# Softmax inverses sent through DRAM as 16 to a partition, more weight sums in the first attention, and block sums stored from ACT's queue

## The chip, the cores and the metric

The kernel runs on one core of one Trainium2 chip. The metric is device time in microseconds (us) of one execution, as the median of several. The core has a matrix engine (TensorE, PE in the profile), three engines for elementwise work (VectorE or DVE, ScalarE or ACT, GpSimd or POOL) and SyncE (SP), which here only issues transfers. Each engine runs its own instructions in order. DMA transfers can be issued by SP, ACT or POOL and run on 16 DMA engines. SBUF is the on-chip memory of 128 partitions, PSUM the accumulators of TensorE, DRAM the memory outside.

## What is computed

All data are float32. Layer 0 is an attention block over four images of 1024 channels by 1024 tokens, with 16 heads of 64; layer 1 is a bottleneck of three convolutions with batch norms and a residual.

```python
# layer 0
qkv = (x @ w_qkv.T + b_qkv).reshape(B, N, 3, nh, hd)
q, k, v = (qkv[:, :, 0], qkv[:, :, 1], qkv[:, :, 2])
q = _apply_rope(q, cos, sin)
k = _apply_rope(k, cos, sin)
q = _rmsnorm(q.reshape(B, N, inner), q_norm_w).reshape(B, N, nh, hd)
k = _rmsnorm(k.reshape(B, N, inner), k_norm_w).reshape(B, N, nh, hd)
scores = jnp.einsum('bqhd,bkhd->bhqk', q, k) * hd ** (-0.5)
attn = jax.nn.softmax(scores, axis=-1)
ctx = jnp.einsum('bhqk,bkhd->bqhd', attn, v).reshape(B, N, inner)
out = _rmsnorm(ctx @ w_proj.T, norm_out_w) + residual
# layer 1
out = jax.nn.relu(_bn(_conv(x, w1, b1, 1, 0), g1, be1))
out = jax.nn.relu(_bn(_conv(out, w2, b2, 1, 1), g2, be2))
out = _bn(_conv(out, w3, b3, 1, 0), g3, be3)
out = jax.nn.relu(x + jax.nn.softplus(residual_scale)[0] * out)
```

## The kernel before

**Stages.** For each image b (0 to 3): project Q, project K, project V, attention, project the context (Y), normalise and store to DRAM. The first convolution of layer 1 is interleaved at the end; the 3x3 convolution (Winograd form) and the third follow. The order on PE, POOL, DVE and ACT is written out by hand: what the program issues in sequence runs in that sequence on each engine. SP's order is arranged by the framework around the waits.

**Strassen sums of weights.** The projections save matmuls by a Strassen-Winograd scheme, which needs sums of blocks of the weights. Q and K of image 0 use one level (`project`): `operands` (L224) loads four 128x512 blocks, makes four sums on DVE (L231 to L234), uses them, and stores the sums to DRAM (L237), as `wd`. All others use two levels (`project2`, L432): their second-level sums are read from DRAM (`wd2`), seven parts for each of WQ, WK, WV and WP. They have to be made once before they are first used: `prepare` (L380) and, for first-level blocks, `prepare_blocks` (L396) load four 128x512 pieces, and a later `make` does four DVE operations of 0.69 us on them and issues four stores from POOL's queue.

**Where these sums are placed.** Beside a projection, `weight_parts(parts, first, step, lag, alloc)` (L935) schedules part i's loads, from POOL's queue, at product number first + i*step, and its `make` lag products later. A product is a group of matmuls; `after(n, step)` runs a step n products on. In the first attention, a list `todo` of such items is worked off: `extra_step` makes the item loaded two steps ago and loads the next, from SP's queue, into four of eight pieces of a ring. In image 3 the same place is taken by the five steps of `filters` (L887 to L915), which make Winograd filter sums: each is a DVE sum (L901), an ACT multiply by 0.5 (L902) and two further DVE operations.

**Attention.** `attention` (L740) is called for the two halves c of the query tokens; each goes over eight pairs of heads hp. For each pair: 32 score matmuls into three PSUM buffers (L757), eight exps on ACT (L764), seven additions on DVE that sum the exps over key blocks (`den`, L766 and L768), 32 matmuls with V (`cx`, L774), and a copy of the result into q's place by ACT (L779). After it come, in this order on DVE: means (L737) where an inverse is ready, a rope turn of K (L694) while some are still waiting, an extra step. After an odd pair eight matmuls with ones (`dn`, L800) sum `den` over the partitions for the two pairs. The reciprocal of `dn` is taken at the start of the next pair (`inverses`, L804 to L815): 128x512 on DVE, of which each row repeats 32 times; four rows go to DRAM (`dens`, a range check reads them at the end), and eight transfers spread the inverses inside SBUF to where `mean_of_v` multiplies them into q at the end of the next odd pair.

**The rule for an extra step** is one at most for each pair, and none beside a rope turn unless the list has become as long as the pairs that are left:

```python
left = (NCH - c) * NHP - hp - 1
turn = bool(waiting)
if turn:
    next_waiting()
if extra and (not turn or len(extra) >= left):
    extra.pop(0)()
```

When attention begins, two rope turns are still waiting in image 0 and four in the others (`rest(leave=...)`, L1014).

Of the kernel before, what the change touches and what calls it, by code (L numbers as in the profile page):

```python
# [11 lines left out]
F32 = mybir.dt.float32  # L12
# [6 lines left out]
P = 128  # L19
B, C, H, W = 4, 1024, 32, 32  # L20
N = H * W
NT = C // P
HD = 64
NHP = C // (2 * HD)
CH = 512
NCH = N // CH
# [8 lines left out]
WQ, WK, WV, WP, W1 = 0, NFB, 2 * NFB, 3 * NFB, 4 * NFB  # L35
# [26 lines left out]
NH = NT // 2  # L62
NG = NT // 2
QH = P // 4
# [21 lines left out]
def program(ctx, tc, x, wblk, w2, w3, vecs, cos, sin, out, bad):  # L86


    nc = tc.nc
# [63 lines left out]
    with tc.tile_pool(name=f"st{u}", bufs=2) as st, ExitStack() as s:  # L153
# [48 lines left out]
        def temp(name):  # L202
            return tmp.tile([P, CH], F32, tag="tmp", name=name)

        def big_temp(name):
            return big.tile([P, N], F32, tag="big", name=name)
# [8 lines left out]
        def flat(t):  # L215
            return t.rearrange("p a b -> p (a b)")
# [7 lines left out]
        def operands(base, g, name):  # L224


            at = base // NT * NG + g
            a11, a12 = (block(base, g, ih, f"{name}_1{ih}") for ih in range(2))
            a21, a22 = (block(base, g + NG, ih, f"{name}_2{ih}") for ih in range(2))
            s1 = chunk(f"w_{name}_s1")  # L230
            nc.vector.tensor_tensor(s1, a21, a22, ALU.add)  # L231
            nc.vector.tensor_tensor(a21, a11, a21, ALU.subtract)
            nc.vector.tensor_tensor(a11, s1, a11, ALU.subtract)
            nc.vector.tensor_tensor(a12, a12, a11, ALU.subtract)  # L234
            spend(4 * TT)
            for o, t in enumerate((a11, s1, a21, a12)):
                nc.gpsimd.dma_start(wd[at, o], flat(t))  # L237
            return [a11, s1, a21, a12, a22]


# [8 lines left out]
        def after(n, step):  # L249
            later.append((pace["at"] + n, step))  # L250
# [486 lines left out]
            nc.vector.tensor_tensor(cx, cx, w, ALU.mult)  # L737
            nc.gpsimd.tensor_scalar(cx, cx, col("bv", hp), None, ALU.add)  # L738

        def attention(b, c, q_all, k_all, v, probs_, late, ready, extra, slow):  # L740


            at = half[c]
            sums_ = []
            for hp in range(NHP):
                n = f"{b}_{c}_{hp}"
                if late:
                    late.pop(0)()
                rows = shifts(q_all, k_all, n, hp, c) if bad is None else None
                probs = []  # L750
                d_ = acc.tile([P, 2, CH], F32, tag="tot", name=f"den_{n}")
                for t in range(N // P):
                    p = probs_[:, t]
                    sc = bank("sc", f"sc_{n}_{t}")
                    for j in range(2):
                        d = slice(j * HD, (j + 1) * HD)
                        nc.tensor.matmul(  # L757
                            sc[:, j], k_all[d, hp, t * P : (t + 1) * P], q_all[d, hp, at],
                            start=True, stop=bad is not None,
                        )  # L760
                    if bad is None:
                        for j in range(2):
                            nc.tensor.matmul(sc[:, j], ones[0:1, :], rows[j], start=False, stop=True)
                    nc.scalar.activation(p, sc, AF.Exp)  # L764
                    if t == 1:
                        nc.vector.tensor_tensor(d_, probs[0], p, ALU.add)  # L766
                    elif t > 1:
                        nc.vector.tensor_tensor(d_, d_, p, ALU.add)  # L768
                    probs.append(p)
                o = bank("cx", f"cx_{n}")  # L770
                for t in range(N // P):
                    for j in range(2):
                        h0 = (2 * hp + j) * HD
                        nc.tensor.matmul(  # L774
                            o[j * HD : (j + 1) * HD, :], v[:, t, h0 : h0 + HD], probs[t][:, j],
                            start=(t == 0), stop=(t == N // P - 1),
                        )

                nc.scalar.copy(q_all[:, hp, at], o)  # L779
                sums_.append(d_)  # L780
                if hp % 2 == 1:
                    for r in ready:
                        mean_of_v(q_all, *r)
                    ready.clear()
                if slow:
                    slow.pop(0)()

                left = (NCH - c) * NHP - hp - 1
                turn = bool(waiting)
                if turn:  # L790
                    next_waiting()
                if extra and (not turn or len(extra) >= left):
                    extra.pop(0)()
                if hp % 2 == 0:
                    continue
                dn = bank("dn", f"dn_{n}")
                for i, d_ in enumerate(sums_):
                    for j in range(2):
                        q = slice((2 * i + j) * QH, (2 * i + j + 1) * QH)
                        nc.tensor.matmul(dn[q, :], ones[:, :QH], d_[:, j], start=True, stop=True)  # L800
                sums_ = []
                late.append(lambda *a, n=n, hp=hp, dn=dn: inverses(b, c, hp, n, dn, ready))

        def inverses(b, c, hp, n, dn, ready):  # L804
            r = temp(f"rec_{n}")
            nc.vector.reciprocal(r, dn)  # L806
            k = 2 * ((b * NCH + c) * NHP + hp - 1)
            if bad is not None:
                nc.sync.dma_start(dens[k : k + 4, :], r[::QH, :])
            w = big_temp(f"inv_{n}")  # L810
            for i in range(2):
                for j in range(4):
                    q = slice((2 * i + j // 2) * QH, (2 * i + j // 2 + 1) * QH)
                    nc.sync.dma_start(w[j * QH : (j + 1) * QH, half[i]], r[q, :])
                ready.append((c, hp - 1 + i, w[:, half[i]]))  # L815

        def o_norm(b, total, ys):
# [117 lines left out]
        def weight_parts(parts, first, step, lag, alloc):  # L935

            for i, part in enumerate(parts):
                after(first + i * step, lambda part=part: after(lag, part(alloc, nc.gpsimd)))

        def pieces_of(tile, cols=NCH):  # L940

            at = deque(tile[:, i, h] for i in range(tile.shape[1]) for h in half[:cols])

            def alloc(name):
                at.rotate(-4)
                return [at[i] for i in range(-4, 0)]

            return alloc
# [28 lines left out]
        for b in range(B):  # L977
# [8 lines left out]
            if b == 0:  # L986
                unused = kp.tile([P, NT, N], F32, tag="k", name="unused")
                parts = blocks_of(WV) + [parts_of[WV][k] for k in (0, 1, 6, 2)]
                weight_parts(parts, 8, 2.4, 4, pieces_of(unused))
            elif b == 1:  # L990
                weight_parts([parts_of[WK][k] for k in (4, 5)], 8.5, 3.5, 3.5, pieces_of(room[:, : NT // 2, :]))
            tq = qk_proj(b, WQ, xs[b], ts[b], "bq", q_all, "q", w1 if b == 0 else None, two, True)
            rope(b, q_all, tq, eps_q, HD / C, None, "q", b == 0)
            k_all = kp.tile([P, NT, N], F32, tag="k", name=f"k_{b}")
# [3 lines left out]
            if b == 0:  # L998
                parts = [parts_of[WV][k] for k in (3, 4, 5)] + [parts_of[WQ][k] for k in (0, 1)]
                weight_parts(parts, 2, 4.5, 4, pieces_of(room))  # L1000
            elif b == 1:
                weight_parts([parts_of[WK][6]], 11, 0, 3.5, pieces_of(room[:, : NT // 2, :]))
            tk = qk_proj(b, WK, xs[b], ts[b], "bk", k_all, "k", None, two)
            rope(b, k_all, tk, eps_rms, 1.0 / C, (wqk_other, wqk), "k")
            v = room
            if b == 0:
                two2 = [None, None, in_place(xs[b], ts[b], room, True)]

                t3 = pieces_of(xs[b][:, :NH, half[1]], 1)
                for k, at, free in ((6, 11, pieces_of(ts[b][1], 1)), (2, 14.5, t3), (3, 18.5, pieces_of(ts[b][1], 1))):  # L1010
                    weight_parts([parts_of[WQ][k]], at, 0, 3.5, free)
            project2(b, 1, WV, *two2[2], b == 0, v, True, "v", lambda c: None)

            rest(leave=4 if b > 0 else 2)  # L1014
# [2 lines left out]
            todo = []  # L1017
            if b == 0:
                todo = blocks_of(WP) + [parts_of[WP][k] for k in (0, 1, 6, 2, 3, 4, 5)]
                todo += [parts_of[WQ][k] for k in (4, 5)] + [parts_of[WK][k] for k in (0, 1)]  # L1020
            made = []

            def extra_step():
# [7 lines left out]
                extra_step()  # L1031
            if b == B - 1:
                extra = filters()
            late, ready = [], []

            def add_residual(f, b=b - 1):
                nc.gpsimd.dma_start(
# [4 lines left out]
            slow = [lambda: None] * 3 + [lambda f=f: add_residual(f) for f in range(NT)] if b > 0 else []  # L1042
            probs_ = xp.tile([P, N // P, 2, CH], F32, tag="x", name=f"p_{b}")
            for c in range(NCH):
                attention(b, c, q_all, k_all, v, probs_, late, ready, extra, slow)
            psum_for("proj")
            room = v_room(f"to_{b}")
            tc_ = [
# [30 lines left out]
                for i in range(NT):  # L1079
                    after(8 + 1.5 * i, lambda i=i: read_back(1, (i,)))  # L1080
            if b == 0:
                weight_parts([parts_of[WK][k] for k in (2, 3)], 6, 7, 4, pieces_of(room[:, 3 * NT // 4 :, :]))
            yt[b] = kp.tile([P, NT, N], F32, tag="k", name=f"y_{b}")
            two = (2, *in_place(q_all, tc_, yt[b], False), True)
            if b + 1 < B:
# [356 lines left out]
```

## Time and profile before

| | |
|---|---|
| median of 3 runs | 2709.47 us (2709.33 to 2710.42) |
| the profiled execution, as timed | 2709.99 us |
| its span, first to last instruction | 2708.20 us |
| TensorE's granted clock, mean | 0.995 |
| DVE reciprocal L806, 128x512 | 3.35 us, 32 times |
| DVE L766 and L768, sums of exps of one pair | 1.20 + 6 x 1.23 us |
| DVE L694, one rope turn | 1.28 + 1.31 us |
| DVE L737, one mean | 0.69 us, 64 times |
| ACT L779, a 128x512 copy | 0.59 us |
| ACT L764, one exp | 1.04 us |
| SP's wait at L809 for the reciprocal | 503.7 us in 25 times |
| SP's loads at L378 waiting for stores into wd2 | 97.9 us in 40 times |

A row of the list of groups gives an engine's busy time and the mean of one instruction. The list of waits gives how long an engine stood still in front of a line, and what came last of what it waited for; an idle engine that is not the bound costs nothing. The timeline gives single instructions, or runs of equal ones, with their starting times. Image 0's Q, K and V take the first 298 us, the first attention lasts to 533 us, and image 3's begins at 2038 us.

### The profile page before, as it was taken

To read this page: it belongs to the slowest core of one execution; us is meant where nothing else is said; L and a number is where in the kernel's file an instruction comes from. 1 tells how busy PE (TensorE), PEld (TensorE's weight loads), DVE (VectorE), ACT (ScalarE), POOL (GpSimd) and SP (SyncE) were. 2 spreads that over 40 slices of the span, in tenths; PEclk is the share of its full clock that TensorE was granted. 3 is DMA by queue.
4 is the path that set the end of the run, shared out by engine and by line. 5 is a ranking of instruction groups with operands and counts; after the bars stand their busy time and mean duration, and the time that the engine had idled before them with its cause. 6 is when DMAs were issued, how large, how long until landed. Compare 5 with 4: busy or idle time off the path is not lost. (4 is left out here: it accounts for less than half of the span.)

```text
span 2708.2 us, 32563 instructions
## 1 busy us (share of the span) xinstructions
PE 2669.3 (99%) x11410; PEld 1659.0 (61%) x11410; DVE 2169.5 (80%) x2516; ACT 1096.1 (40%) x1520; POOL 452.6 (17%) x552
## 2 busy tenths in 40 slices
PE   9999999999999999999999999999999999999997
PEld 4448533488888333688886333888884335746843
DVE  4577899998887977888878877987888878646987
ACT  2222455523342555333343555233525553312266
POOL 2562222322011211100111211100111211000000
PEclk9999999999999999999999999999999999999999
DMA  7897755587677341456765420665783314662165
GB/s 272 317 306 214 230 154 165 167 269 246 197 203 213 62 92 32 148 152 222 188 189 144 88 54 17 214 205 173 189 233 79 75 36 132 196 240 86 63 227 209
DMA packets 245964, 453.54 MB, mean 167 GB/s; under 512 B 28384, under 2 KB 117264, under 8 KB 245792
## 3 DMA queue, kind: packets, MB, share of 16 engines
q1 hardware_dynamic: 203568, 310.72, 36.5%
q0 software_dynamic: 42224, 140.63, 19.6%
q8 instruction: 94, 1.54, 0.2%
q14 instruction: 78, 0.64, 0.1%
HBM read 316.71 MB, written 96.78 MB: 153 GB/s over the span
## 5 line engine op out<-in xcount | busy, mean ns | idle before, releaser
L768 DVE TENSOR_TENSOR den<-den,p 128x1024 f32<-128x1024 f32 x384 | 470.5, 1225 | 40.7 <-DVE den L768 0.9
L764 ACT ACTIVATE p<-sc 128x1024 f32<-128x1024 f32 x512 | 476.3, 1043 | 55.0 <-PE sc L757 54.8
L757 PE MATMUL sc<-q,k 64*128 64x512 f32 x2048 | 457.7, 596 | 0.0
L757 PEld LDWEIGHTS sc<-q,k 64*128 64x128 f32 x2048 | 189.9, 186 | 265.6 <-issue 121.2
L774 PE MATMUL cx<-p,to 128*64 128x512 f32 x1536 | 340.2, 595 | 0.0
L774 PEld LDWEIGHTS cx<-p,to 128*64 128x64 f32 x1536 | 106.0, 137 | 228.3 <-issue 228.3
L738 POOL TENSOR_SCALAR q<-q,vec 128x512 f32<-128x512 f32 x64 | 127.0, 1989 | 559.2 <-DVE q L737 559.2
L453 PE MATMUL p_v<-w_v,x 128*128 128x256 f32 x928 | 210.8, 380 | 1.3 <-DVE x L424 1.3
L458 PE MATMUL p_y<-q,w_y 128*128 128x256 f32 x928 | 210.1, 380 | 1.1 <-DMA w_y<-wdf 1.1
L458 PEld LDWEIGHTS p_y<-q,w_y 128*128 128x128 f32 x928 | 175.9, 190 | 28.5 <-issue 4.8
L453 PEld LDWEIGHTS p_v<-w_v,x 128*128 128x128 f32 x928 | 176.9, 191 | 26.8 <-DVE x L424 2.1
L779 ACT COPY q<-cx 128x512 f32<-128x512 f32 x64 | 37.5, 587 | 356.9 <-PE cx L774 356.9
L458 PE MATMUL p_k<-to,w_k 128*128 128x256 f32 x672 | 154.8, 384 | 4.7 <-ACT to L547 4.7
L458 PE MATMUL p_q<-to,w_q 128*128 128x256 f32 x672 | 152.5, 380 | 0.7 <-ACT q L512 0.6
L458 PEld LDWEIGHTS p_k<-to,w_k 128*128 128x128 f32 x672 | 127.9, 192 | 26.3 <-ACT to L547 7.1
L458 PEld LDWEIGHTS p_q<-to,w_q 128*128 128x128 f32 x672 | 127.2, 190 | 20.2 <-ACT q L512 1.9
L766 DVE TENSOR_TENSOR den<-p 128x1024 f32<-128x1024 f32 x64 | 76.5, 1195 | 77.3 <-ACT p L764 77.3
L806 DVE RECIPROCAL rec<-dn 128x512 f32<-128x512 f32 x32 | 107.2, 3352 | 20.6 <-PE dn L800 20.6
L774 PE MATMUL cx<-p,rq 128*64 128x512 f32 x512 | 113.4, 595 | 0.0
L1346 PE MATMUL c<-h,w 128*128 128x512 f32 x256 | 110.3, 592 | 0.9 <-ACT h L1248 0.9
L700 POOL DMA_DIRECT2D k<-ks x64 | 56.1, 1036 | 278.2 <-ACT p L764 111.0
L453 PE MATMUL p_v<-w_v,t 128*128 128x256 f32 x384 | 92.0, 385 | 3.6 <-DMA w_v<-in_wblk_dram 3.6
(444 smaller groups left out, 4188.0 us busy)
## 6 DMA issues: line engine op xcount, KB each, us to landing
w_v<-wd2f SPq DMA_DIRECT2D x112, 256.0 KB
w_y<-wd2f SPq DMA_DIRECT2D x112, 256.0 KB
w_q<-wd2f SPq DMA_DIRECT2D x84, 256.0 KB
w_k<-wd2f SPq DMA_DIRECT2D x84, 256.0 KB
x<-in_x_dram SPq DMA_DIRECT2D x64, 256.0 KB
q<-qs POOLq DMA_DIRECT2D x64, 256.0 KB, 5.7
k<-ks POOLq DMA_DIRECT2D x64, 256.0 KB, 4.5
inv<-rec SPq DMA_DIRECT2D x256, 64.0 KB
```

The lines of the kernel that those rows point to most:

```text
L453: nc.tensor.matmul(o[:, q].rearrange("p (g f) -> p g f", g=2), r[:, i, q * P : (q + 1) * P], wt[:, :, i, :], skip_group_check=True, **at,)
L458: nc.tensor.matmul(o[:, q], wt[:, q, i, :], r[:, i, :], skip_group_check=True, **at)
L700: nc.gpsimd.dma_start(dst[i::2, f, :], other[1 - i :: 2, :], accum_op=ALU.add)
L738: nc.gpsimd.tensor_scalar(cx, cx, col("bv", hp), None, ALU.add)
L757: nc.tensor.matmul(sc[:, j], k_all[d, hp, t * P : (t + 1) * P], q_all[d, hp, at], start=True, stop=bad is not None,)
L764: nc.scalar.activation(p, sc, AF.Exp)
L766: nc.vector.tensor_tensor(d_, probs[0], p, ALU.add)
L768: nc.vector.tensor_tensor(d_, d_, p, ALU.add)
L774: nc.tensor.matmul(o[j * HD : (j + 1) * HD, :], v[:, t, h0 : h0 + HD], probs[t][:, j], start=(t == 0), stop=(t == N // P - 1),)
L779: nc.scalar.copy(q_all[:, hp, at], o)
L806: nc.vector.reciprocal(r, dn)
L1346: nc.tensor.matmul(os[i], w3t[k][f // NH][:, f % NH, :], h2[b, k][:, half[c]], start=(k == 0), stop=(k == NPT - 1),)
```

## The change

1. `inverses`: except for the last pair of an image (c = 1, hp = 7), where the code is as before, `dn` is copied to SBUF by ACT, not inverted; its four distinct rows go to DRAM, and from there come back as 128x16 (`few`). At the end of the same even pair (`half_done`) DVE inverts these, they go back to DRAM, and eight transfers broadcast them to 32 partitions each (`spread`).
2. The extra steps are spread evenly over the 15 slots of the 16 pairs of an attention, beside rope turns too. The first attention has 20 items for 15: WQ 3 and WK 6, 2, 3, 4 come in. With 20 items slots 0, 3, 6, 9 and 12 have two steps each. The five filter steps of image 3 come at slots 0, 3, 6, 9, 12.
3. Fewer parts beside projections: none beside Q and K of image 1, two beside V of image 0 (three before), one beside Y of image 0 (two before).
4. The four stores of `operands` come one product later, and from ACT's queue.

```diff
             spend(4 * TT)
-            for o, t in enumerate((a11, s1, a21, a12)):
-                nc.gpsimd.dma_start(wd[at, o], flat(t))
+
+            def keep():
+                for o, t in enumerate((a11, s1, a21, a12)):
+                    nc.scalar.dma_start(wd[at, o], flat(t))
+
+            after(1, keep)
             return [a11, s1, a21, a12, a22]
...
                     ready.clear()
+                if half_done:
+                    half_done.pop(0)()
                 if slow:
                     slow.pop(0)()
 
-                left = (NCH - c) * NHP - hp - 1
-                turn = bool(waiting)
-                if turn:
+                if waiting:
                     next_waiting()
-                if extra and (not turn or len(extra) >= left):
+                slots = NCH * NHP - 1
+                for _ in range(len(extra) - steps_in_all * max(slots - 1 - c * NHP - hp, 0) // slots):
                     extra.pop(0)()
...
+        half_done = []
+
         def inverses(b, c, hp, n, dn, ready):
+
+
             r = temp(f"rec_{n}")
-            nc.vector.reciprocal(r, dn)
             k = 2 * ((b * NCH + c) * NHP + hp - 1)
-            if bad is not None:
+            if (c, hp) == (NCH - 1, NHP - 1):
+                nc.vector.reciprocal(r, dn)
                 nc.sync.dma_start(dens[k : k + 4, :], r[::QH, :])
+                spread(c, hp, n, ready, [r[q * QH : (q + 1) * QH, :] for q in range(4)])
+                return
+            nc.scalar.copy(r, dn)
+            nc.sync.dma_start(dens[k : k + 4, :], r[::QH, :])
+            few = st.tile([P, 4 * CH // P], F32, tag="few", name=f"few_{n}")
+            rows = dens[k : k + 4, :].rearrange("r (a t) -> (r a) t", t=4 * CH // P)
+            nc.sync.dma_start(few, rows)
+
+            def invert():
+                nc.vector.reciprocal(few, few)
+                nc.sync.dma_start(rows, few)
+                spread(c, hp, n, ready, [dens[k + q, :].partition_broadcast(QH) for q in range(4)])
+
+            half_done.append(invert)
+
+        def spread(c, hp, n, ready, rows):
             w = big_temp(f"inv_{n}")
             for i in range(2):
                 for j in range(4):
-                    q = slice((2 * i + j // 2) * QH, (2 * i + j // 2 + 1) * QH)
-                    nc.sync.dma_start(w[j * QH : (j + 1) * QH, half[i]], r[q, :])
+                    nc.sync.dma_start(w[j * QH : (j + 1) * QH, half[i]], rows[2 * i + j // 2])
                 ready.append((c, hp - 1 + i, w[:, half[i]]))
...
-            elif b == 1:
-                weight_parts([parts_of[WK][k] for k in (4, 5)], 8.5, 3.5, 3.5, pieces_of(room[:, : NT // 2, :]))
             tq = qk_proj(b, WQ, xs[b], ts[b], "bq", q_all, "q", w1 if b == 0 else None, two, True)
...
-            elif b == 1:
-                weight_parts([parts_of[WK][6]], 11, 0, 3.5, pieces_of(room[:, : NT // 2, :]))
             tk = qk_proj(b, WK, xs[b], ts[b], "bk", k_all, "k", None, two)
...
-                t3 = pieces_of(xs[b][:, :NH, half[1]], 1)
-                for k, at, free in ((6, 11, pieces_of(ts[b][1], 1)), (2, 14.5, t3), (3, 18.5, pieces_of(ts[b][1], 1))):
-                    weight_parts([parts_of[WQ][k]], at, 0, 3.5, free)
+                weight_parts([parts_of[WQ][k] for k in (6, 2)], 11.5, 6.5, 4, pieces_of(ts[b][1], 1))
...
-                todo += [parts_of[WQ][k] for k in (4, 5)] + [parts_of[WK][k] for k in (0, 1)]
+                todo += [parts_of[WQ][k] for k in (3, 4, 5)] + [parts_of[WK][k] for k in (0, 1, 6, 2, 3, 4)]
...
-                weight_parts([parts_of[WK][k] for k in (2, 3)], 6, 7, 4, pieces_of(room[:, 3 * NT // 4 :, :]))
+                weight_parts([parts_of[WK][5]], 8, 0, 4, pieces_of(room[:, 3 * NT // 4 :, :]))
```

More of the change, by code (lines that the diff above doesn't have):

```diff
@@ L738, in mean_of_v, with attention @@
             nc.gpsimd.tensor_scalar(cx, cx, col("bv", hp), None, ALU.add)
-        def attention(b, c, q_all, k_all, v, probs_, late, ready, extra, slow):
+        def attention(b, c, q_all, k_all, v, probs_, late, ready, extra, slow, steps_in_all):
             at = half[c]
@@ L1033, in program @@
                 extra = filters()
-            late, ready = [], []
+            late, ready, steps_in_all = [], [], len(extra)
             def add_residual(f, b=b - 1):
@@ L1044, in program @@
             for c in range(NCH):
-                attention(b, c, q_all, k_all, v, probs_, late, ready, extra, slow)
+                attention(b, c, q_all, k_all, v, probs_, late, ready, extra, slow, steps_in_all)
             psum_for("proj")
```

## The prediction

> **What bounds the kernel now.** I read the busy table first, then TensorE's waits, then the stages that these waits name on the timelines, each engine apart.
>
> ```profile
> PE 2669.3 (99%) x11410; PEld 1659.0 (61%) x11410; DVE 2169.5 (80%) x2516; ACT 1096.1 (40%) x1520; POOL 452.6 (17%) x552
> ```
>
> TensorE is busy for all but 39 us, and the change leaves its instructions and their order alone. Only the gaps, and the slow matmuls behind a gap, can move. In the list of TensorE's waits (total, times, longest) the reader is to see five that matter:
>
> ```profile
> PE pa_q L298 <- DMA x<-in_x_dram: 5.9, 1, 5.9
> PE p_k L458 <- ACT to L547: 4.7, 6, 2.4
> PE p_v L453 <- DMA w_v<-in_wblk_dram: 3.6, 1, 3.6
> PE pa_k L298 <- DVE w_k_3b L233: 2.0, 1, 2.0
> PE p_q L458 <- DMA w_q<-wdf: 0.8, 2, 0.6
> PE pa_k L298 <- DVE w_k_2b L233: 0.6, 1, 0.6
> ```
>
> On TensorE's timeline (start, length, shape, count) a gap has a second price: the row behind it runs slower.
>
> ```profile
> 163.49 3.60 PE L298 MATMUL pa_k<-t,w_k_1b 128*128 128x512 f32 x8
> 187.13 5.40 PE L298 MATMUL pa_k<-t,w_k_3b 128*128 128x512 f32 x8 [1.99 <-DVE w_k_3b L233]
> 278.28 3.78 PE L453 MATMUL p_v<-w_v,t 128*128 128x256 f32 x8 [3.59 <-DMA w_v<-in_wblk_dram]
> 1333.23 1.89 PE L458 MATMUL p_k<-to,w_k 128*128 128x256 f32 x8
> 326.61 2.18 PE L800 MATMUL dn<-den,ones 128*32 128x512 f32 x8
> 357.07 1.07 PE L800 MATMUL dn<-den,ones 128*32 128x512 f32 x8
> ```
>
> Eight matmuls of 512 columns take 3.60 at pace and 5.40 after an idle 1.99; eight of 256 take 1.89 and 3.78. The first dn of image 0 takes 2.18 where the next takes 1.07: it already waits inside for its second operand. VectorE explains it, and what stands in front of the K sums:
>
> ```profile
> 182.15 0.69 DVE L387 TENSOR_TENSOR rq<-rq 128x512 f32<-128x512 f32 x1 [5.73 <-DMA rq<-in_wblk_dram]
> 319.81 7.87 DVE L768 TENSOR_TENSOR den<-den,p 128x1024 f32<-128x1024 f32 x6
> 2052.66 1.28 DVE L694 SCALAR_TENSOR_TENSOR ks<-k,wqk_other,sinT 128x1024 f32<-128x1024 f32 x1
> 2053.97 1.28 DVE L694 SCALAR_TENSOR_TENSOR k<-k,wqk,cosT 128x1024 f32<-128x1024 f32 x1
> 2053.17 7.44 ACT L764 ACTIVATE p<-sc 128x1024 f32<-128x1024 f32 x8 [0.47 <-PE sc L757]
> 298.00:533.00 235.00, 234.93 (x1090) 84.07 (x1088) 221.27 (x203) 129.83 (x145) 65.98 (x82) 1.00 0.54 164
> ```
>
> The last row is the first attention: length, busy time of PE, weight loads, DVE, ACT, POOL, clock, DMA share, GB/s. VectorE has 14 us to spare in 235 there, TensorE nothing.
>
> **What the Trainium skill says.** "TensorE: Matmul & The Clock Gate", What's actually happening: an idle window of some 3.4 us halves the clock, and about as much activity restores it. By that a restart costs up to 1.7 us; the trace has 1.8 after 1.99 idle and 2.8 after 3.59, so I use the trace. "DMA: Bandwidth & Descriptors", Anatomy of one DMA: about 2 us fixed, plus bytes at 436 GB/s; here the 4 KB copy inv_d<-rms lands in 2.1 us, and busy windows reach 300 to 330 GB/s. The same page, Issuing engines are not separate DMA queues: a transfer moved to another engine shares the same 16 DMA engines. The trace before has no such pair to compare. The same page, Two DMAs through the same engine are not ordered: a read-back must wait on the write's semaphore, so DRAM round trips add up.
>
> **The change part by part.** Gains first; what a gap costs is its idle time plus the slow rows behind it.
>
> K of image 0. The loads and stores of five weight parts share POOL's queue there with the operands' stores (L237). These leave it for ACT's, and the loads that were queued behind them issue earlier, so the 5.73 us wait ahead of L387 shrinks and the sums of w_k_3b (L231 to 234, 4 x 0.69) follow earlier. TensorE's idle 0.6 and 2.0, and slow rows of 1.8 and some 0.2, make 4.6. I take -4.5, bounds 0 (the DMA engines, 0.93 busy from 104 to 206 us, set the landing) and -5.0. ACT's 32 issues (about 0.5 us each, as SP's rows show) stand one product behind the sums; the next copy that TensorE needs from ACT is three products of 1.8 us away: nothing, 1 us if VectorE is that late.
>
> V of image 0. Two of three weight parts remain (1 MB of loads at 260 us and its 1 MB of stores vanish). The wait is 3.59, its slow rows 1.9 + 0.9: 6.4. I take -5.5, bounds -2 (the remaining parts collide) and -6.4.
>
> Image 1: K loses part 6, whose four sums (2.9 us) stand ahead of the adds that ACT's copy into "to" waits for. 2.35 idle and slow rows of 1.5, and smaller ones, make 4.7, of which images 2 and 3, which have no such part, keep 1.5: -3.2 (-2.5 to -3.5). Q loses parts 4 and 5: two waits of w_q, 0.8, one of ACT, 0.6, their slow rows 0.4: -1.8 (-0.5 to -2). Y of image 0 has one part for two: half of its 1.1 us wait, -0.6 (-1.2 to +1).
>
> These sum to -15.6.
>
> First attention, first slot. Twenty steps over fifteen slots put two makes (2 x 2.9) into slot 0 for one, on VectorE between den of pair 0 and den of pair 1. Before, den of pair 1 ended at 327.68 (319.81 + 7.87) while dn began at 326.61. So no slack is left: 2.9 more idle, with slow rows of 2, +4.9 (+2.9 to +5.5). The other double slots have cover: den ends about 12.25 us after its pair's first score, dn comes at 14.1, and the reciprocal of 3.35 that stood in front of an even pair's sums is gone. Sum of VectorE there: 221.3 - 8 x 3.2 + 5 x 2.9 = 210, under before.
>
> Image 3's filters. Their five steps went to slots without a rope turn; now they come at slots 0, 3, 6, 9, 12, besides turns. A step is a VectorE sum (L901), then an ACT multiply (L902, 0.63) in ACT's order ahead of the next pair's first exp. At slot 0 the turn ends at 2055.2 (2053.97 + 1.28), the sum at 2055.9, the multiply at 2056.5: the exp that began at 2053.17 is 3.3 late. Behind it stand the seven other exps, and TensorE's fourth score waits for a score buffer. With 0.4 slack: 2.9 idle and 2 slow, +4.9. At slot 3 means (1.3), turn and sum end 16.8 after the pair's start, where the exp wants 16.3: with the multiply 1.8 late, +1.9. At 6 nothing; at 9 and 12 as before. Sum +6.8 (+4 to +8).
>
> Start. POOL's eight free loads (2 MB at about 331 GB/s, 6 us of DMA) no longer queue behind the operands' stores: they issue at once and share the engines, 0.93 busy in the first 25 us, with x and the weights. First matmul +0.6, the S2 weights +0.7: +1.3 (+0.3 to +4).
>
> Inverses. Twenty-eight reciprocals of 3.35 become 28 copies of 0.59 on ACT, 28 reciprocals of 128x16 (no such row; 0.1 to 0.3, below by the fixed part of short rows) and two more DRAM steps. ACT's copy lies between dn's end and the first exp, 1 us apart: 0. VectorE's 88 us saved are off the path: 0. What is at risk is VectorE's wait for "few": behind it stand means, turn, makes and the next den. Few needs two transfers of 2 us after SP comes to it; SP's loads ahead wait for the stores of the last makes (97.9 us in 40 waits). Counted from the even pair's first score: the odd pair's make ends at about 0 (12.25 + 2.9 after its own start, 15.1 before), its stores land 2.8 later (median of wd2f<-w_pre), the four loads waiting for them take SP about 2, the rec store and few 2.1 each plus 0.5 for issue: 10 behind a single step, and 2.9 more, 13, behind a double. VectorE gets there at 12.25; the even pair has no dn, so some 3.9 more is covered. I take +0.3, bounds 0 and +27.
>
> Losses: 4.9 + 6.8 + 1.3 + 0.3 = 13.3. Net -2.3. The profiled execution took 2709.99 (span 2708.20 and 1.79 around it), so 2707.7 for such a one; the median of the runs, 2709.47, lies 0.5 lower: 2707.2.
>
> **Rivals.** About 0.2%, 5.4 us, is what a measurement here can tell from no change.
>
> R1, the covers hold: the double make and the filter sums fit because the reciprocals are gone from VectorE. For it: 88 us freed. Against: in slot 0 of both attentions no reciprocal has come yet. -15.6 + 1.6 = -14.0: 2695.5.
>
> R2, slower: "few" lands too late in the first attention. Place: VectorE's new wait at the end of even pairs, behind SP's loads. It decides from 16.2 us (12.25 + 3.9) after the even pair's first score. If it came at 18.3, 2.1 idle and 1.7 slow would be paid seven times, +27: 2734. For it: SP's waits for stores reach 11 us. Against: DMA share is only 0.54 there.
>
> R3, the stalls in K and V of image 0 stay because the DMA engines, not a queue's order, set the landing: 9.9 of the gain missing, 2717.1. For it: shares of 0.93. Against: 2 MB fewer around V, and loads at the start that come 30 us earlier.
>
> R4, the change does nothing it says: SP spreads its order so that all waits stay as they were; 2709.5. The freed early loads speak against it.
>
> **How the numbers follow.** Forecast 0.42, R1 0.22, R2 0.15, R3 0.17, R4 0.04. The forecast's own range is 2701 to 2713: an eighth of it lies past the 5.4 us on either side. Faster: R1 and a tenth of the forecast, 0.26. Slower: R2, R3 and 0.01, 0.33. Same: 0.41. The range, 2695 to 2723, holds the forecast, R3 and most of R1, and leaves out R2 and R1's far end.
>
> **What would show it.** Right: no 3.59 wait of w_v, and pa_k on w_k_3b at 3.60; dn at about 330 with a gap before it; the exps of image 3's second pair starting at about 2056 on a clock shifted by the earlier gains, with TensorE idle on ACT; small waits of VectorE on few. Wrong: a wait of L387 still near 5 us in K (R3); waits on few of several us in every even pair (R2); neither first slot with a gap (R1). A first matmul later than 8 us would make the start the mis-sized term.

## The result, and the profile after

The changed kernel takes 2710.64 us (median of 20 runs, 2707.76 to 2713.54), the kernel before 2706.27 (20 runs, 2702.14 to 2710.42). The ratio is 1.0015, with an interval from 1.0008 to 1.0021: about 4 us slower, which is a small but real loss, and less than the 0.2% that I had called no change. The three runs shown ahead of the prediction (2709.33 to 2710.42) lay at the upper end of what the kernel before does. Beside the experiments it ran 96 times more, in three groups with medians of 2706.96 to 2707.59; against these the loss is 3.1 to 3.7 us.

The busy table and the list of TensorE's waits of the changed kernel (total, times, longest):

```profile
PE 2669.2 (99%) x11410; PEld 1655.8 (61%) x11410; DVE 2085.5 (77%) x2516; ACT 1111.2 (41%) x1548; POOL 415.9 (15%) x500
```

```profile
PE pa_q L302 <- DMA x<-in_x_dram: 7.5, 2, 5.8
PE dn L805 <- DVE den L772: 4.8, 3, 2.9
PE p_k L462 <- ACT to L551: 3.2, 6, 0.8
PE pa_k L302 <- DVE w_k_3b L233: 1.9, 1, 1.9
PE p_y L462 <- DMA w_y<-wdf: 1.7, 2, 1.4
```

VectorE lost 84 us of work and TensorE none, as foreseen. The wait of p_v for w_v (3.6 before) has left the head of the list; dn waiting for den, which the list before did not have, has come in, and the wait for x has a second part.

TensorE's timeline of the changed kernel (start, length, shape, count, idle time before it and what ended it) shows the new gaps at the start, in the first attention's first pair, and in its third dn:

```profile
5.78 2.04 PE L302 MATMUL pa_q<-x,w_q 128*128 128x512 f32 x2 [5.78 <-DMA x<-in_x_dram]
9.55 15.47 PE L302 MATMUL pa_q<-x,w_q 128*128 128x512 f32 x30 [1.73 <-DMA x<-in_x_dram]
...
321.43 1.05 PE L805 MATMUL dn<-den,ones 128*32 128x512 f32 x4
325.33 1.92 PE L805 MATMUL dn<-den,ones 128*32 128x512 f32 x4 [2.85 <-DVE den L772]
...
385.05 1.05 PE L805 MATMUL dn<-den,ones 128*32 128x512 f32 x4
387.76 1.05 PE L805 MATMUL dn<-den,ones 128*32 128x512 f32 x4 [1.66 <-DVE den L772]
```

The first matmul comes on time, the third does not: 1.73 idle. In dn the first four matmuls (pair 0 or 4) run, then the other four wait for the den of the odd pair. At 325 us they also run at half pace, 1.92 for 1.05. That second part does not come each time: behind the same gap of 2.85 us they took 1.92 again in the second profile of the changed kernel, and 1.05 in two of the kernels below.

**Where the time went, stage by stage.** Below, the time that TensorE lost in each stage, in us: from the stage's first matmul to the next stage's first, less the number of matmuls of each shape times the spacing at which that shape runs undisturbed in these traces (429 ns for 512 columns, 216 for 256, 221 for scores, 219 for cx, 125 for dn). Idle time and slow matmuls behind it are both in it. The unchanged kernels were profiled more than once: before three times, after twice.

```
                          start  K b0   V b0  attn b0  Y b0  Q,K b1  all lost
before                     2.4    4.8    6.9    1.5    1.5     7.7    39.7
before, second profile     3.1    5.4    6.6    1.5    1.9     8.5    41.0
before, third profile      2.1    2.9    5.5    1.5    1.0     8.1    35.4
after                      5.3    2.3    1.5   10.4    2.3     2.5    39.2
after, second profile      5.6    2.5    1.7   10.0    3.3     2.5    40.1
stores on POOL             2.6    5.0    0.6   11.0    2.3     2.5    43.6
first slot single          4.9    4.7    1.7    6.2    3.8     2.5    38.8
few by POOL                4.6    2.4    1.1    9.5    2.7     2.5    36.6
even doubles               5.1    3.0    1.8    2.7    0.9     2.5    30.6
even doubles, held start   2.2    1.9    1.5    2.1    2.0     2.5    28.4
old inverses               5.4    2.9    2.4   15.3    3.4     2.5    47.9
even doubles, held start,
  old inverses             3.1    2.8    1.5   12.3    3.6     2.5    40.5
```

From the mean of before to the mean of after: start +2.9, K -2.0, V -4.7, first attention +8.7, Y +1.3, image 1 -5.6. What the change gains beside the projections it gives back in the first attention and at the start. All stages together the profiles differ by +1.0 (39.7 less 38.7), and the medians by 4.4. Single runs of one kernel spread over 8 us, and the three profiled executions of before took 2705.7 to 2711.3, so the 3 us between are not placed in a stage.

### The profile page after: what moved, and what is told of

Read it like the earlier page. It is cut to its first block, busy times and chain, and to the rows that moved or that the text cites. A ratio compares the mean times of both kernels' runs of the same rounds, so it can differ in the third digit from the quotient of the medians.

```text
span 2707.7 us, 32716 instructions
## 1 busy us (share of the span) xinstructions
PE 2669.2 (99%) x11410; PEld 1655.8 (61%) x11410; DVE 2085.5 (77%) x2516; ACT 1111.2 (41%) x1548; POOL 415.9 (15%) x500
## 5 line engine op out<-in xcount | busy, mean ns | idle before, releaser
L462 PE MATMUL p_y<-to,w_y 128*128 128x256 f32 x384 | 90.2, 379 | 0.3 <-DMA w_y<-wdf 0.3
```

Of the source, the lines that this page charges most:

```text
L462: nc.tensor.matmul(o[:, q], wt[:, q, i, :], r[:, i, :], skip_group_check=True, **at)
```

## The experiments

**The kernel before, profiled again**, no edit.

> The kernel before once more, unchanged, for a second profile. The profiled execution of before took 2709.99 us, but the median of its 20 runs is 2706.27. Theory: the wait of w_v in image 0 (3.6 us idle, 6.4 with slow rows) differs from execution to execution, and in one of about 2706 us it is under 2 us with its rows near pace. Rival: w_v waits 3.6 us again, and the 3 to 4 us are missing at another place (the K sums w_k_3b, or the first matmul).

It took 2711.31, so it was no typical execution either. In the list of TensorE's waits three of the load stalls differ from the first profile: the wait for w_k_3b is 3.0 for 2.0, that for w_v 2.8 for 3.6, and that for w_q of image 1 2.2 for 0.8. The theory is not settled by it, so here is a third profile.

> The kernel before once more, unchanged, for a third profile. Two profiled executions took 2709.99 and 2711.31 against a median of 2707.6 over 43. Theory: executions differ by 2 to 5 us in the stalls where loads collide (start, w_k_3b, w_v, w_q and w_k of image 1), of which the changed kernel has only the first two; one near the median shows a smaller sum of the last three than 11.2 us (first profile) and 15 us (second). Rival: these stalls are the same size and the other places, outside the stages that the change touches, differ.

It took 2705.70. K lost 2.9 here, against 4.8 and 5.4; V 5.5 against 6.9 and 6.6; the stalls of image 1 were 8.1, no smaller. The last three stalls that the expectation names (w_v, and w_q and w_k of image 1) lie in the columns V b0 and Q,K b1 of the table. These sum to 13.6, against 14.6 and 15.1; the 11.2 and 15 of the expectation were put together from the largest rows alone. So the theory holds for K and, less, for V, and fails for image 1. The price that I put on the K stall was that of an execution in which it was large.

**The changed kernel, profiled again**, no edit.

> The changed kernel once more, unchanged, for a second profile, since the three profiles of before differ by up to 5.6 us. Theory: the losses of the first attention (10.2 us in the first profile, of which 5.3 at the first dn) and at the start (5.3) are there again within 1 us each, while the K stall may be anything from 2 to 4.6: 2709 to 2713. Rival: the attention's losses vary as the load collisions do, and are under 7 or over 13 us here.

2710.32. Start and attention are there again (5.6 and 10.0), within 0.4 us of the first profile. They belong to the kernel and not to one execution.

**Stores on POOL's queue.**

```diff
-            def keep():
-                for o, t in enumerate((a11, s1, a21, a12)):
-                    nc.scalar.dma_start(wd[at, o], flat(t))
-            after(1, keep)
+            for o, t in enumerate((a11, s1, a21, a12)):
+                nc.gpsimd.dma_start(wd[at, o], flat(t))
```

> The changed kernel with the four stores of the block sums issued from POOL's queue at once, as before. Theory: the second gap of 1.7 us at the start (after two matmuls) and its slow rows go, because POOL's eight free loads stand behind the first stores again: -3 us; the wait in K of image 0 grows from 1.9 us idle to about 2.0 + 0.6 with slow rows: +2.5. Net -0.5, 2710. Rival: the gap at the start comes from how the loads of x happen to land; it stays, and only the K loss comes back: 2713.

2711.15, ratio to before 1.0012 (1.0005 to 1.0018): no different from the changed kernel. The two halves are as the theory has them: the start falls from 5.3 to 2.6, K rises from 2.3 to 5.0. For the start the rival falls: over all profiles it lost 4.6 to 5.6 us in the six in which ACT issues the first stores, and 2.1 to 3.1 in the six in which POOL does. For K one profile says less, since another with ACT's stores lost 4.7 (the next kernel). POOL's timelines show the cause at the start, in the changed kernel:

```profile
1.95 3.73 POOL L405 DMA_DIRECT2D unused<-in_wblk_dram  x7
```

and in the kernel before:

```profile
32.20 0.57 POOL L237 DMA_DIRECT2D wdf<-w_q_0b  x1 [30.25 <-DVE w_q_0b L233]
...
34.36 2.13 POOL L401 DMA_DIRECT2D unused<-in_wblk_dram  x4
```

With no store ahead of them, loads first used at 50 us issue at 2 us, between the loads of x. So part 4 of the change costs 2.7 us at the start, and what it gains in K is no more than that. In this profile image 3's V also lost 6.5 us (1.6 in before's), behind one wait of 4.3 us that no other profile has; it is why this profile's sum is high.

**One item in the first slot.**

```diff
-                for _ in range(len(extra) - steps_in_all * max(slots - 1 - c * NHP - hp, 0) // slots):
+                slot = c * NHP + hp
+                if b == 0:
+                    steps = 2 if slot in (3, 6, 9, 12, 14) else 1
...
+                for _ in range(min(steps, len(extra))):
```

> The changed kernel with one item, not two, in the first slot of the first attention; the fifth double slot is slot 14 instead (slots 3, 6, 9, 12, 14). Theory: dn of the first pair loses 1.1 us against 4.8 + 0.5, so -4.2 us: 2706.4; slots 3 and 9 go on losing 2.7 and 1.3. Rival: VectorE is only later elsewhere, because the sums made are the same number in the same time; the loss moves to the end of the attention (sums of the context, w_y), and the time stays near 2710.

2708.58, ratio 1.0004 (0.9996 to 1.0012). On TensorE's timeline the first dn is as before the change:

```profile
323.77 2.18 PE L810 MATMUL dn<-den,ones 128*32 128x512 f32 x8
```

The attention lost 6.2 instead of 10.4, which is the 4.2 expected there. The rival may have a small part: Y lost 3.8, against 2.3 and 3.3 in the changed kernel's profiles. In the time only 2 us came of it, not 4.2, with an interval that overlaps the changed kernel's; K lost 4.7 in this profile.

**Few through POOL's queue.**

```diff
-            nc.sync.dma_start(dens[k : k + 4, :], r[::QH, :])
+            nc.gpsimd.dma_start(dens[k : k + 4, :], r[::QH, :])
...
-            nc.sync.dma_start(few, rows)
+            nc.gpsimd.dma_start(few, rows)
```

> The changed kernel with the store of the four rows and the read-back of few issued from POOL's queue instead of SP's. Theory: few was late at pair 4 of the first attention (VectorE idle 4.9 us) because SP issued it behind loads that wait for the stores of two makes. From POOL's queue it waits for no load: VectorE's wait for few falls from 13.6 us in all to under 3, dn at 385 and at 476 us lose nothing, -4 us: 2706.6. Rival: few is late because the stores and read-backs themselves take long beside 256 KB transfers; then the wait stays at 10 us or more and the time at 2710. Second rival: POOL's own queue (stores of makes) holds it as long.

My theory failed. In the first attention VectorE's wait for few fell only from 13.6 us to 12.5, in six times each; another 12.0 came in images 1 to 3, where no attention lost more than in the changed kernel. At pair 4 VectorE still waited 3.8, and besides the first dn three more lost 2.1, 1.6 and 1.3 us. POOL's timeline gives one half of the reason:

```profile
357.58 4.33 POOL L396 DMA_DIRECT2D wd2f<-w_pre  x8
361.90 0.58 POOL L822 DMA_DIRECT2D densf<-rec  x1
368.08 0.57 POOL L825 DMA_DIRECT2D few<-densf  x1 [5.61 <-DMA densf<-rec]
```

ACT had finished the copy of dn at 355.6. Its store stood behind the eight stores of the two makes until 361.9. This is the second rival. The view of DMA issues of this kernel from 350 to 376 us (size, median us from issue to landing) gives the other half:

```profile
wd2f<-w_pre POOLq DMA_DIRECT2D x9, 256.0 KB, 3.6
w_pre<-in_wblk_dram SPq DMA_DIRECT2D x4, 256.0 KB, 6.1
w_pre<-wdf SPq DMA_DIRECT2D x4, 256.0 KB, 5.7
densf<-rec POOLq DMA_DIRECT2D x1, 8.0 KB, 5.9
few<-densf POOLq DMA_DIRECT2D x1, 8.0 KB, 4.9
```

Eight stores and eight loads of 256 KB surround two transfers of 8 KB, and each of these takes about as long as its neighbours. No load stood ahead of few in POOL's queue, and yet the first of its two trips alone landed 6 us after its issue. So the first rival holds as well: the transfers themselves are slow beside big ones. The Trainium skill ("DMA: Bandwidth & Descriptors", Issuing engines are not separate DMA queues) says that starting DMAs on several engines saves only the time that it takes to start them. The two trips agree with it: from POOL's queue they took 5.9 and 4.9 us, against a median of 1.9 for few over the whole kernel. The wait in an engine's queue comes on top, 6.3 us here. The time, 2710.06, ratio 1.0008 (1.0000 to 1.0016), is not apart from the changed kernel's.

**Double steps at even pairs.** The edit is that of the single first slot, with the slots (4, 6, 8, 10, 12).

> The changed kernel with the five double slots of the first attention at even pairs (slots 4, 6, 8, 10, 12) and one item in every other slot. Theory: few is late where a double step comes just ahead of it, at the end of an odd pair: the 2 MB stored and the 2 MB loaded by two makes fill the DMA engines while few makes its two DRAM trips. With doubles at even pairs only 1 MB each way is ahead of few. VectorE's wait for few falls from 13.6 us to under 6, every dn of the first attention loses under 0.5 us but the first (1.1): -8 us against the changed kernel, ratio to before 0.998 to 0.999 (2702 to 2704). Rival: a double step at an even pair costs its 2.9 us at the next dn, since den is summed behind it: dn after slots 4, 6, 8, 10, 12 each lose 1 to 2 us, and the time stays at 2709 to 2711.

2700.82, ratio 0.9977 (0.9971 to 0.9984): 9.8 us under the changed kernel, and faster than before. The attention lost 2.7 instead of 10.4 and Y 0.9 instead of 2.3, and VectorE waited for few 4.1 us in all. Of the attention's gain some 4 us are the first slot, as in the single first slot; the rest comes with the other double steps. VectorE's timeline at slot 4 shows why a double step costs nothing here:

```profile
365.60 0.24 DVE L833 RECIPROCAL few<-few 128x16 f32<-128x16 f32 x1
365.76 0.63 DVE L391 TENSOR_TENSOR w_pre<-w_pre,w_pre 128x512 f32<-128x512 f32 x1
...
370.66 0.69 DVE L394 TENSOR_TENSOR w_pre<-w_pre,w_pre 128x512 f32<-128x512 f32 x1
371.26 1.22 DVE L770 TENSOR_TENSOR den<-p 128x1024 f32<-128x1024 f32 x1
372.59 7.88 DVE L772 TENSOR_TENSOR den<-den,p 128x1024 f32<-128x1024 f32 x6
```

and TensorE's, that dn finds den done:

```profile
381.50 1.07 PE L810 MATMUL dn<-den,ones 128*32 128x512 f32 x8
```

Few is there when VectorE comes to it; the two makes (365.8 to 371.3) fill time before the next den, which ends at 380.5, a microsecond ahead of dn. The rival (1 to 2 us at each of the five) falls: one dn lost 1.1, one 0.3, and the others nothing beyond the first's old 1.1.

**Double steps at even pairs, with the start held back.** To the slots of the last kernel comes this:

```diff
-            def keep():
+            def keep(queue=nc.scalar):
                 for o, t in enumerate((a11, s1, a21, a12)):
-                    nc.scalar.dma_start(wd[at, o], flat(t))
-            after(1, keep)
+                    queue.dma_start(wd[at, o], flat(t))
+            if at == 0:
+                keep(nc.gpsimd)
+            else:
+                after(1, keep)
```

> The kernel of e5 with the first four stores of block sums (WQ, block 0) on POOL's queue again, so that POOL's eight free loads stand behind them; the other 28 stores stay on ACT's. Theory: no gap after two matmuls at the start, 2.4 us less there (2.5 lost instead of 4.9) and the K stall as in the changed kernel (2.2 to 4.6): 2.4 us below e5, 2700 to 2702. Rival: the loads held back collide later, with the weights of Q or K, and the K stall grows by as much.

2698.95, ratio 0.9975 (0.9967 to 0.9983). The start lost 2.2 instead of 5.1, K 1.9; in the profile the theory is right and the rival not. The times of this kernel and the last are not safely apart: their medians differ by 1.9 us, and their intervals overlap. Both are faster than the kernel before and the changed kernel.

**The old inverses, with 20 items.**

```diff
-            if (c, hp) == (NCH - 1, NHP - 1):
+            if True:
                 nc.vector.reciprocal(r, dn)
```

> The changed kernel with all inverses taken as before: one 128x512 reciprocal on VectorE, spread inside SBUF; 20 items in the first attention as in the change. Theory: with 20 items VectorE has 221 + 15 = 236 us of work in 235, and the reciprocal stands at the start of even pairs, which have the room; dn is late after the double steps at odd pairs, by about what few costs now, so 2709 to 2713, within 3 us of the changed kernel: part 1 buys next to nothing. Rival: without part 1 VectorE falls behind pair after pair and every dn loses 2 to 3 us: 2720 or more.

2718.58, ratio 1.0045 (1.0032 to 1.0059), 7.9 us above the changed kernel. Neither is right in size: I had said within 3 us, the rival 2720 or more from every dn. Five of the eight dn lost 2 to 6 us, with the scores behind them. Of the loss, 5 us lie in the attention (15.3 against 10.2). That is what part 1 is worth there at these slots, after what few costs.

**The old inverses, with double steps at even pairs and the start held back**, the slots and the queue of the kernel with the held start, and the edit of the old inverses.

> The kernel of e6 (double slots at even pairs, held start) with the inverses as before, on VectorE and spread inside SBUF. Theory: part 1 is what gives VectorE the room for five more items; without it the double steps (5.8 us) and the 3.35 us reciprocal come in the same even pairs, and dn after slots 4, 6, 8, 10, 12 waits: 1.5 to 2.5 us each, 8 to 12 us over e6, 2707 to 2711, about the time of before. Rival: the placement at even pairs does it all, and the reciprocals are covered: within 3 us of e6, 2699 to 2702.

2711.21, ratio 1.0014 (1.0006 to 1.0021), 12.3 us above its twin with the new inverses; the theory said 8 to 12. The attention lost 12.3 for 2.1. The placement alone does not do it, nor do the inverses alone: an even pair has room for two makes only when the 3.35 us reciprocal is gone from it.

## Why the prediction was wrong

I forecast -2.3 us, and the sign was wrong. The time, 2710.64, is 3.4 above the forecast and within the stated range, but that is partly luck: I counted from the 2709.47 of three runs, and from the median of all 20, 2706.27, the same change would have given 2704.0.

Five terms came out worse than forecast. The largest error among them is in the step on the inverses: I put each DRAM trip of few at 2.1 us, and behind the double step of slot 3 they took 4.8 to 6.0. The step on the filters failed too, in the other direction: the wait that I priced at 6.8 us does not exist. Term by term, against the means of the stage table and the first dn's own rows:

- K of image 0: -4.5 forecast, -2.0 measured; the range of the term (0 to -5) held it. The first half of the step was right: VectorE's wait ahead of L387 (L391 now) was 5.2 to 6.7 us in the four profiles with POOL's stores and 2.7 to 3.8 in the eight with ACT's. The second half was not: the sums of w_k_3b did not follow earlier by as much, because they now wait for their own blocks, which they did not before. VectorE's list of waits in the changed kernel has it:

```profile
DVE w_k_3b_s L231 <- DMA w_k_3b<-in_wblk_dram: 1.7, 1, 1.7
```

So TensorE's idle time in K fell only from 2.7 us to 1.9 (means). The other 1.2 us are slow matmuls. Those of the w_k_3b row came behind 1.99 and 3.00 us of idle time in two profiles of before (5.40), and not behind 1.46 in the third or 1.91 and 1.92 in the changed kernel's two (3.70). But the length of the gap does not settle it: behind 2.60 the row took 5.40 in the kernel with the single first slot, and behind 2.57 it took 3.70 in the last experiment. In all, the eight profiles with ACT's stores lost 1.9 to 4.7 us in K (mean 2.8), and the four with POOL's 2.9 to 5.4 (mean 4.5). R3 came in part: the landing of loads still sets the end of this wait. Whether the DMA engines, at 0.92 in this stage, or the order of the loads holds them back was not tried.
- V of image 0: -5.5 forecast, -4.7 measured. Image 1's Q and K: -5.0 forecast, -5.6 measured. Right in size. No run takes part 3 back by itself, but all nine profiles with it lost 0.6 to 2.4 in V and 2.5 in image 1, and the three without it 5.5 to 6.9 and 7.7 to 8.5.
- Y of image 0: -0.6 forecast, +1.3 measured; outside the range that I gave by a little. Y lost 0.9 to 2.0 in the profiles whose attention lost under 3 us, and 2.3 to 3.8 in all others, so the late VectorE is the likely cause; the part itself was not tried alone.
- First slot: +4.9 forecast. The first dn and the scores behind it lost 5.3 us against 1.3 before, +4.0; with the single first slot they lost 1.1. Right.
- Filters of image 3: +6.8 forecast, +0.1 measured. This step was wrong in its reason. I had the ACT multiply (L902, L926 now) wait for the VectorE sum ahead of it. It multiplies another block, which is loaded long before; only the operation after it needs both. ACT's timeline of the changed kernel, and below it VectorE's, show it:

```profile
2052.30 0.63 ACT L926 ACTIVATE t_w<-t_w 128x512 f32<-128x512 f32 x1
2052.87 7.44 ACT L768 ACTIVATE p<-sc 128x1024 f32<-128x1024 f32 x8
```

```profile
2054.88 0.68 DVE L925 TENSOR_TENSOR t_w<-t_w 128x512 f32<-128x512 f32 x1
```

The multiply starts 2.6 us before the sum, and the exps begin at once behind it. The code said so: g1 is scaled, new is summed.

- Start: +1.3 forecast, +2.9 measured, within its bounds. The place was missed: the first matmul was not late but the third was, by 1.73 us, and slow matmuls follow.
- Inverses: +0.3 forecast, +4.7 measured (the attention's 8.7 less the first slot's 4.0). This is the largest error on the side of the losses. VectorE's timeline of the changed kernel at pair 4, behind the double step of slot 3:

```profile
362.81 7.88 DVE L772 TENSOR_TENSOR den<-den,p 128x1024 f32<-128x1024 f32 x6
375.61 0.25 DVE L828 RECIPROCAL few<-few 128x16 f32<-128x16 f32 x1 [4.92 <-DMA few<-densf]
```

and SP's, over the same time:

```profile
361.95 0.55 SPq L822 DMA_DIRECT2D densf<-rec  x1
362.59 3.18 SPq L382 DMA_DIRECT2D w_pre<-in_wblk_dram  x3
365.87 3.73 SPq L382 DMA_DIRECT2D w_pre<-wdf  x4
369.65 0.46 SPq L825 DMA_DIRECT2D few<-densf  x1
```

Pair 4's first score starts at 356.88. Counted from there, my sum had the store issued at 7.7 (2.9 + 2.8 + 2), few at 10.3, and few landed at 13. Measured are 5.1, 12.8 and 18.7. My 16.2 for the point from which it costs was good: few came 2.5 us beyond it, and dn lost 2.7. What was mis-sized was the DRAM trip: I took 2.1 us for each, from the median of 4 KB copies, most of which ran with the DMA engines 0.5 to 0.6 busy, and leaned on a mean DMA share of 0.54 over the stage. From the store's issue to few's the share was 1.00 here, since a double step brings its 4 MB exactly then. Few took 6.0 us from issue to use. The 7.7 us between the two issues are not the store's trip alone, since SP issued seven loads in them; from POOL's queue, without loads between, that trip took 5.9. R2 thus happened, once with 2.7 us (1.8 in the second profile) and once with 1.3 to 1.6, both after double steps at the end of odd pairs; two more dn lost 0.4 to 0.7. Seven times full price it was not.

R1 did not come. It put the filters at no cost, which came true, but not for its reason, the freed VectorE. R4 fell. One reading of the chances was wrong as well: the forecast's own range ends at 2713, 3.5 above 2709.5, so no part of it lies 5.4 us above.

The terms as measured sum to +0.7, which is 3.0 from the forecast. That it is so near is luck: the filters' error of -6.7 hid most of the other errors, which sum to +9.7. Most of the rest of the measured 4.4 us lies in which executions were profiled: the three of the kernel before took 2709.0 on average, 2.7 above its median, and the two of the changed kernel 2709.9, 0.7 below its own.

## What to carry to other kernels

Price a small transfer that stands in a chain by what lands beside it in those microseconds, not by the stage's mean load; and put bursts of large transfers where the chain isn't. Behind a wait that shrinks look for the next one, which may end hardly earlier. Before costing a wait, read in the code which operand the waiting instruction takes. Stalls in which loads collide differ from one execution to the next, so a gain read from one profile of them is worth its mean over several.

## What the runs showed of the hardware

Three transfers of 8 KB took 4.9 to 6.0 us while sixteen of 256 KB were under way, one issued by SP and two by POOL, against a median of 1.9 for such a transfer over a whole kernel. A reciprocal of 128x16 takes 0.25 us, where 128x512, with 32 times the elements, takes 3.35.

Matmuls behind a gap can run slower, and the length of the gap alone does not decide it: eight of 128x512 took 5.40 us behind an idle 1.99 or 2.60, and 3.70 behind 2.57.

Run by run, one kernel on one core spread over 4 to 11 us. Between the three profiles of the kernel before, which lost 35.4 to 41.0 us, most of the difference was in the stages where DMA loads are the last to arrive.
